# Two layer borders of a four-layer convolution kernel: the last image's stores, its norm, and the pools' waits

## Chip, cores and metric

The kernel runs on one core of a Trainium2 chip, as one launch. The metric is device time in microseconds (us) of one execution; lower is better. Before the change, three runs gave 5763.12, 5770.26 and 5770.41 us, median 5770.26.

TensorE is called PE below (its weight loads PEld), VectorE DVE, ScalarE ACT, GpSimd POOL; SP is the engine whose queue issues nearly all of this kernel's transfers (DMAs).

## The reference

Four layers run one after the other on x of shape 32 x 96 x 56 x 56 (images, channels, rows, columns), in float32. Each takes the group norm of x (32 groups of 3 channels, over the 3 channels and all pixels of one image), applies a block, and adds the result to x:

```python
def _gn(v, G=32, eps=1e-5):
    ...
    m = jnp.mean(g, axis=(2, 3, 4), keepdims=True)
    s = jnp.var(g, axis=(2, 3, 4), keepdims=True)
    return ((g - m) / jnp.sqrt(s + eps)).reshape(v.shape)
...
x = x + _L0_conv_ref(_gn(x), ...)   # 1x1 to 576 channels, SiLU, 3x3 depthwise, SiLU, squeeze-excite, 1x1 to 96, + identity
x = x + _L1_conv_ref(_gn(x), ...)   # 5x5 depthwise plus three Haar wavelet levels, each with 5x5 depthwise, and inverse
x = x + _L2_conv_ref(_gn(x), ...)   # 4-bit quantized: 1x1 to 576, 3x3 depthwise, 1x1 to 96
x = x + _L3_conv_ref(_gn(x), ...)   # 9x9 depthwise with diffusion kernels
```

## The kernel before, in words

**Two kinds of layer.** Layers 0 and 2 go image by image: an image is a tile of 96 channels (partitions) by 3136 pixels, two images stand side by side in a pair tile `xt` of 25 KB a partition. Layers 1 and 3 go channel by channel: a channel's tile `X` holds all 32 images, with 112 partitions for row and phase in each of two halves and 16 more for the rows beside them (`load_halves`, L657). Depthwise filters become products with banded matrices: `raw` is read from memory and put in order by ACT copies into `T` (L666, L694). So at the two borders 0 to 1 and 2 to 3 the data change from images to channels through memory (`y0`, `y2`), in six arrays of 16 channels each (GR = 16). No channel can be read before the last image of its group of 16 is stored; and the factors of the group norm (a row of 32 scales, 32 offsets and a bias for each channel) need the statistics of all 32 images.

**The end of layers 0 and 2.** `store_images` (L159) stores two images at once, one DMA for each group of 16 channels. The last image is stored by tiles: four tiles of 14 rows, six groups, 24 DMAs of 49 KB (`store_tile`, L152), issued by `add` (L495, L1171) when a tile's residual is added. A row piece of one image is 14 floats, 56 B. Then `store_norm` (L95) makes the factors for all 32 images: statistics of the last image (layer 0: ACT sums with an accumulator, L309, and L508 to L524; layer 2: `bn_stats` on DVE, L87), group means by a product with `S.grp` on PE (L106), variances by a second (L111), a power on POOL (L113), and the row is stored in memory by SP (L119).

**The beginning of layers 1 and 3.** `layer1` (L710) loads constants, lets POOL clear its T3, T2 and c2 tiles (L749), and runs over 48 pairs of channels; iteration i loads pair i + 3 (`load`, L752: X, the norm row `nr` broadcast to all partitions, raw, raw2 and T3), prepares pair i + 2 (`normal`, `matrices1`, `matrices2`, `high`, `low`), takes pair i + 1 through the small wavelet levels (`lowest1`, `lowest2`, `level3`, `level2`), and finishes pair i (`level1`, L835: two coarse and three fine matmuls into one PSUM tile for each half, then DVE adds and SP stores to `y1`). `layer3` (L1247) does the same with single channels, loading four ahead (AHEAD), preparing two ahead, and filtering the current one with three matmuls a half (`filtered`, L1280).

**What sets the order.** In layers 0 and 2 the order of PE, DVE and ACT work is written out by hand (L62, L68: a letter for each step, `-` and `+` for an image earlier or later), while SP's and POOL's order is chosen by the compiler's scheduler. In the loops of layers 1 and 3 SP's order is that of the program too (`MANUAL_SP`). Every engine works through its queue in order, so a waiting instruction holds all that stands behind it.

**Memory.** Each layer takes its tiles from pools that are opened when it begins and closed when it ends, so a later layer's pools lie where those of an earlier one lay. Before the change, the first use of the new pool's space waits for the whole of what was there. In layer 0 the pair of images 30 and 31 lies in `pairs[1]` (L546); layer 2 begins its own pairs in `Layer2` (L890), which also prepares its weights while layer 1 runs (`behind`, L1348).

## Time and profile before

| what | value |
|---|---|
| median of the runs | 5770.26 us (5763.12 to 5770.41) |
| the profiled execution | 5772.8 us, of which the profile's span is 5771.0 us |
| busy in the span: PE, DVE, ACT, POOL | 5488.4, 4689.3, 4184.5, 239.8 us |
| mean granted PE clock | 0.982 of full speed |
| HBM read and written | 284.44 and 214.08 MB |
| chain of work that ended last, by engine | PE 82%, DMA 5%, ACT 4%, issue 3%, DVE 3%, SP 1%, POOL 1% |

The page cuts the span into 40 slices of 144 us; a digit is the busy share in tenths:

```profile
PE   5999999999999999995999999999999999997999
...
PEclk9999999999999999997999999899999999998999
DMA  3122333332222233216566666579688696845888
GB/s 99 17 56 59 63 57 59 57 58 56 42 54 54 58 59 58 47 20 66 142 148 148 148 148 113 21 53 50 42 52 46 51 54 42 53 28 35 241 254 245
```

From left to right: the start, layer 0 to slice 19, layer 1 to slice 25, layer 2 to slice 37, layer 3 to the end. PEclk is the clock that was granted to PE. The DMA row is the mean busy share of the 16 DMA engines. Rows of other views give a start, a length and what ran; a bracket at the end gives the idle time ahead of the instruction and what ended it. SPq rows are SP's queue: the length is the time that issuing took, not the transfer's.

### The profile page before, as it was taken

What the parts mean: (1) busy time and instruction counts of PE and PEld (TensorE: products, weight loads), DVE (VectorE), ACT (ScalarE), POOL (GpSimd) and SP (SyncE); (2) the same over time, 40 slices, a digit from 0 to 9 for tenths busy, and PEclk for the clock granted to TensorE, in tenths of its full rate; (3) what the DMA queues carried; (4) which work ended last, traced back from release to release, by engine and by line L of the source; (5) the groups of instructions that cost most, each with busy time, mean ns of one, the idle gap of its engine ahead of it and who ended that gap; (6) DMA issues with size and microseconds to landing.
All of it is one profiled execution on the core that took longest, in us unless ns stands there. A gap on an engine that the chain in (4) does not pass through costs nothing.

```text
span 5771.0 us, 137224 instructions
## 1 busy us (share of the span) xinstructions
PE 5488.4 (95%) x59688; PEld 3064.9 (53%) x59688; DVE 4689.3 (81%) x5388; ACT 4184.5 (73%) x6036; POOL 239.8 (4%) x156
## 2 busy tenths in 40 slices
PE   5999999999999999995999999999999999997999
PEld 2333333333333333332566665777788778775444
DVE  6999999999999999994776665777777777774777
ACT  5888888888888888874565554777777777774555
POOL 5000000000000000000000000000000000000000
PEclk9999999999999999997999999899999999998999
DMA  3122333332222233216566666579688696845888
GB/s 99 17 56 59 63 57 59 57 58 56 42 54 54 58 59 58 47 20 66 142 148 148 148 148 113 21 53 50 42 52 46 51 54 42 53 28 35 241 254 245
DMA packets 1306412, 454.32 MB, mean 79 GB/s; under 512 B 1123841, under 2 KB 1301753, under 8 KB 1303889
## 3 DMA queue, kind: packets, MB, share of 16 engines
q1 hardware_dynamic: 1305809, 445.54, 50.9%
q8 instruction: 468, 7.67, 0.6%
q14 instruction: 135, 1.11, 0.1%
HBM read 284.44 MB, written 214.08 MB: 86 GB/s over the span
## 4 chain that ended last, share of the span: by engine, by line
PE 82%; DMA 5%; ACT 4%; issue 3%; DVE 3%; SPq 1%; POOL 1%; POOLq 0%; ACTq 0%; DVEq 0%
PE psd L432 17%; PE psd L1131 12%; PE psj L483 11%; PE ps L365 7%; PE pc L842 7%; PE ps L1112 6%; PE pse L388 6%; PE pc L1285 4%; PE psj L1168 3%; PE pc L826 2%; ACT hi L1084 2%; PE pa L800 2%; DMA xt<-y 1%; PE pc L816 1%; DMA X<-y 1%
## 5 line engine op out<-in xcount | busy, mean ns | idle before, releaser
L406 DVE SCALAR_TENSOR_TENSOR h<-hpad,l_wdw,h 128x3136 f32<-128x3136 f32 x512 | 1782.3, 3481 | 9.1
L432 PE MATMUL psd<-plane,filt 128*32 128x392 f32 (+5 forms) x16384 | 1082.9, 485 | 0.0
L1131 PE MATMUL psd<-apad,diag 64*64 64x392 bf16 x20736 | 913.2, 329 | 68.3 <-issue 64.6
L1131 PEld LDWEIGHTS <-diag 64*64 64x64 bf16 x20736 | 686.4, 106 | 291.1 <-issue 114.7
L432 PEld LDWEIGHTS psd<-plane,filt 128*32 128x32 f32 (+1 forms) x16384 | 389.9, 108 | 674.4 <-issue 621.5
L672 ACT COPY T<-raw 32x112 f32<-32x112 f32 (+2 forms) x1440 | 463.0, 385 | 270.6 <-DMA raw<-tdiff 217.1
L1102 ACT ACTIVATE u<-ps,o,s 128x784 int16<-128x784 f32 x576 | 538.1, 1002 | 165.7 <-PE ps L1112 146.8
L1102 ACT ACTIVATE a<-psd,o,s 128x784 int16<-128x784 f32 x448 | 423.9, 998 | 273.7 <-PE psd L1131 273.7
L365 PE MATMUL ps<-xn,l_wboth 96*128 96x392 f32 (+1 forms) x1536 | 465.0, 505 | 23.9 <-ACT xn L347 23.0
L406 DVE SCALAR_TENSOR_TENSOR hc<-hhalf,l_wdw,hc 128x1568 f32<-128x1568 f32 x256 | 473.7, 1851 | 16.1 <-ACT hc L399 9.5
L1112 PE MATMUL ps<-hi,l_w1q 96*128 96x392 f32 x1280 | 467.3, 365 | 9.2 <-ACT hi L1084 9.2
L1285 PE MATMUL pc<-x,T 128*112 128x416 f32 (+1 forms) x1152 | 416.0, 524 | 41.9 <-DMA raw<-tdiff 40.0
L842 PE MATMUL pc<-x,T 128*112 128x416 f32 (+1 forms) x1152 | 445.4, 523 | 0.0
L1112 PE MATMUL ps<-lo,l_w1q 96*128 96x392 f32 x1280 | 442.7, 346 | 0.0
L388 PE MATMUL pse<-xn,l_wboth 96*32 96x392 f32 x4096 | 392.0, 501 | 3.6 <-ACT hab L409 3.6
L365 PEld LDWEIGHTS ps<-xn,l_wboth 96*128 96x128 f32 (+1 forms) x1536 | 219.0, 172 | 248.6 <-issue 59.8
L1285 PEld LDWEIGHTS pc<-x,T 128*112 128x112 f32 x1152 | 204.3, 178 | 253.0 <-issue 229.8
L409 ACT ACTIVATE hab<-psd,o,s 128x784 f32<-128x784 f32 x256 | 283.8, 1113 | 57.8 <-PE psd L432 54.8
L375 ACT ACTIVATE hpad<-ps,o,s 128x784 f32<-128x784 f32 x256 | 278.6, 1104 | 48.9 <-PE ps L365 47.5
L483 PE MATMUL psj<-h,wg 128*32 128x392 f32 x3072 | 307.1, 514 | 1.3 <-DVE wg L472 1.3
L483 PE MATMUL psj<-hab,wg 128*32 128x392 f32 x3072 | 304.1, 509 | 0.0
L392 ACT ACTIVATE plane<-pse,o,s 128x784 f32<-128x784 f32 x256 | 256.0, 1000 | 25.4 <-PE pse L388 20.4
(234 smaller groups left out, 7618.9 us busy)
## 6 DMA issues: line engine op xcount, KB each, us to landing
X<-y SPq DMA_DIRECT2D x192, 392.0 KB
y<-xt SPq DMA_DIRECT2D x180, 392.0 KB
xt<-in_x_dram SPq DMA_DIRECT2D x16, 2352.0 KB
y<-y SPq DMA_DIRECT2D x96, 392.0 KB
xt<-y SPq DMA_DIRECT2D x96, 392.0 KB
out_dram<-y SPq DMA_DIRECT2D x96, 392.0 KB
twav<-zwav SPq DMA_DIRECT2D x768, 36.8 KB
raw<-twav SPq DMA_DIRECT2D x96, 168.0 KB
```

What stands on the lines that cost most here:

```text
L365: nc.tensor.matmul(ps[p, j, :NT], wexp[:, k * 128 : k * 128 + 128][:, m], im["xn"][:, j, rows, :].rearrange("c h w -> c (h w)"), start=Tru ...
L388: nc.tensor.matmul(ps[f * GC : (f + 1) * GC, half, :NT].rearrange("p (r w) -> p r w", w=W2), wexp[:, c : c + GC], im["xn"][:, f % 2, r0 : ...
L406: nc.vector.scalar_tensor_tensor(h2, taken(im, k, t), wdw[:, k, t : t + 1], h2, ALU.mult, ALU.add)
L409: nc.scalar.activation(view, ps, AF.Silu, bias=bi[1][:, c : c + 1], scale=sc[1][:, c : c + 1], accum_out=accum)
L432: nc.tensor.matmul(ps[at * GC : (at + 1) * GC, r, :NT].rearrange("p (r w) -> p r w", w=W2)[:, r0 - half * n : r1 - half * n, q0:q1], filt[ ...
L483: nc.tensor.matmul(ps[s * GC : (s + 1) * GC, t, :NT].rearrange("c (m r q) -> c r q m", m=2, q=W4), wg[p, k, c * GC : (c + 1) * GC], phases ...
L672: nc.scalar.copy(to.rearrange("x t (p s) -> x t p s", p=NPH), v[:, k])
L842: nc.tensor.matmul(ps[:PH, to], st["T"][j][:, h, k, :], st["x"][:, j, h, of], start=False, stop=(n == NK - 1))
L1102: nc.scalar.activation(out, ps, AF.Identity, bias=o[:, c : c + 1], scale=s[:, c : c + 1])
L1112: nc.tensor.matmul(ps[:, j, :NT], w1[:, k * 128 : k * 128 + 128], im[part][:, r0 : r0 + RT, :].rearrange("c h w -> c (h w)"), start=(part ...
L1131: nc.tensor.matmul(ps[q, j, :NT].rearrange("p (r w) -> p r w", w=W), diag[p, k, t, :], v, start=(t == 0), stop=(t == 8))
L1285: nc.tensor.matmul(ps[:, :, to], st["T"][:, h, k, :], st["x"][:, h, :, of], start=(n == 0), stop=(n == NK - 1))
```

## The change

It does five things, at both borders where not said otherwise.

- **Stores.** Of the last image's 24 store DMAs, those of channel group 0 are issued first (in layer 0 two of them, in layer 2 three, by `add`; the rest of group 0 ahead of the next layer's first X). All others are kept in a list (`LastStores`) in the order of the groups, and `left.issue(n)` takes n of them from it between the next layer's loads: 2 and then 3 in each `load` of layer 1; 1 and then 2 behind each channel's loads, from channel 2 on, in layer 3.
- **Norm.** `store_norm` becomes a class `Norm`: the factors of images 0 to 30 (EARLY) are made while the last image is still worked on, those of image 31 (LATE) at the end. In layer 0 the last image's statistics are taken by `bn_stats` on DVE, tile by tile, in place of the ACT sums; in layer 2 they are taken tile by tile too. The row is stored by `made.store` within the next layer's loads.
- **Pair 0 of layer 1.** Its matrices are loaded before its images. A new `begin` prepares it in one piece and lets PE make its fine matmuls at once; its `level1` then adds only the coarse ones. Iteration -2 does nothing beside it. The constants are loaded inside the loop's hand-set order. In layer 3 the matrices of channels 0 and 1 are loaded first.
- **Memory.** The pair tile with the last image and the norm row stay in a pool of their own (`kept`) through layers 1 and 2, where they serve as layer 2's first pair and its norm row. The three sets of T3, T2 and c2 are placed in reverse.
- **Waits.** The pools of layers 1, 2 and 3 are opened with `reuse_waits="tile"`: a tile of a new pool waits for the tiles that lay where it lies, not for the whole pool.

The diff, cut to its core (left out: signatures, the other pools' same argument, the unpacking of names):

```diff
+def tile_stats(nc, st, x, i):
+
+    for j in (2 * i, 2 * i + 1):
+        nc.vector.bn_stats(st[:, j, :], x[:, j * RT * NPH : (j + 1) * RT * NPH, :])
+
+
+EARLY, LATE = slice(0, B - 1), slice(B - 1, B)
+
+
+class Norm:
+
+
+    def __init__(self, nc, S, room, row, mv, bias):
+        self.nc, self.S, self.mv, self.bias = nc, S, mv, bias
+        self.d, self.dv, self.ve = (room[:C, i * B : (i + 1) * B] for i in range(3))
+        self.row = row[:C]
+
+    def slices(self, at):
+        return [t[:, at] for t in (self.d, self.dv, self.ve, self.row[:, :B])]
+
+    def means(self, at):
+        self.nc.vector.tensor_copy(self.slices(at)[2], self.mv[:, at, 0])
+
+    def centred(self, at, ps):
+
+        nc = self.nc
+        d, dv, ve, _ = self.slices(at)
+        ps = ps[:C, 0, : d.shape[-1]]
+        nc.tensor.matmul(ps, self.S.grp, ve, start=True, stop=True)
+        nc.vector.tensor_tensor(d, ve, ps, ALU.subtract)
+        nc.vector.tensor_tensor(dv, d, d, ALU.mult)
+        nc.vector.tensor_tensor(dv, dv, self.mv[:, at, 1], ALU.add)
+        nc.vector.tensor_tensor(d, ve, d, ALU.subtract)
+
+    def deviations(self, at, ps):
+
+        nc = self.nc
+        _, dv, ve, rstd = self.slices(at)
+        ps = ps[:C, 1, : ve.shape[-1]]
+        nc.tensor.matmul(ps, self.S.grp, dv, start=True, stop=True)
+        nc.vector.tensor_scalar(ve, ps, EPS_GN, None, ALU.add)
+        nc.gpsimd.tensor_tensor(rstd, ve, self.S.mhalf[:C, : ve.shape[-1]], ALU.pow)
+
+    def begin(self):
+        if self.bias is None:
+            self.nc.vector.memset(self.row[:, 2 * B :], 0.0)
+        else:
+            self.nc.vector.tensor_copy(self.row[:, 2 * B :], self.bias)
+        self.means(EARLY)
+
+    def last(self, ps):
+        self.means(LATE)
+        self.centred(LATE, ps)
+        self.deviations(LATE, ps)
+        self.nc.vector.scalar_tensor_tensor(self.row[:, B : 2 * B], self.d, -1.0, self.row[:, :B], ALU.mult, ALU.mult)
+
+    def store(self, dram):
+        self.nc.sync.dma_start(dram, self.row)
...
+def store_tile(nc, y, xt, i, g):
 
     rows = slice(i * 2 * RT * NPH, (i + 1) * 2 * RT * NPH)
-    for to, of in groups(im["xt"][:, rows], y, lambda y: y[:, rows, im["b"], :], store=True):
+    for to, of in groups(xt[:, rows], y, lambda y: y[:, rows, B - 1, :], store=True, of=[g]):
         nc.sync.dma_start(to, of)
+
+
+class LastStores:
+
+
+    def __init__(self, nc, y, xt, first):
+        self.left = [(lambda i=i, g=g: store_tile(nc, y, xt, i, g)) for g in range(C // GR)
+                     for i in range(NP) if g or i in first]
+
+    def issue(self, n):
+        for store in self.left[:n]:
+            store()
+        del self.left[:n]
...
         im["wg"] = wg
+        if im["b"] == B - 1:
+            norm.begin()
         nc.vector.tensor_tensor(im["wg"], wproj, im["gate"].unsqueeze(2).to_broadcast([128, ND, C]),
                                 ALU.mult)
+        if im["b"] == B - 1:
+            norm.centred(EARLY, pn)
...
+        if (im["b"], i) == (B - 1, 0):
+            norm.deviations(EARLY, pn)
...
-                        store_tile(nc, y0, im, 2 * t + a)
+                        tile_stats(nc, stats, im["xt"], 2 * t + a)
+                        if a == 0:
+                            store_tile(nc, y0, im["xt"], 2 * t, 0)
 
...
     def store(im):
+        if im["b"] == B - 1:
+            nc.vector.bn_aggr(mv_all[:, B - 1, :], stats.rearrange("c a b -> c (a b)"))
+            norm.last(pn)
+            return
...
-    cp = ctx.enter_context(tc.tile_pool(name="l1c", bufs=1))
+    cp = ctx.enter_context(tc.tile_pool(name="l1c", bufs=1, reuse_waits="tile"))
...
+    sets = [None] * NF
+    for i in reversed(range(NF)):
+        sets[i] = {
+            name: cp.tile(shape, dtype, tag=f"{name}{i}", name=f"{name}{i}") for name, shape, dtype in (
+                ("T3", [2 * HH, 2, HH * KW], F32), ("T2", [PH, 2, NK, 128], F32), ("c2", [128, 2, 2, N2, B], F32R))}
+    for d in sets:
+        for t in d.values():
+            nc.gpsimd.memset(t.bitcast(F32) if t.dtype == F32R else t, 0.0)
...
+        if i == 0:
+            for c in range(2):
+                matrices(c)
+            left.issue(2)
+            made.store(norm)
+            for part in (images, factors):
+                for c in range(2):
+                    part(c)
+            return st
+        for c in (2 * i, 2 * i + 1):
+            images(c)
+            factors(c)
+            matrices(c)
+        left.issue(3)
...
+    def fine(st, j, h, first):
+        ps = st["pf"][j, h]
+        for n, (k, to, of) in enumerate(shifts(W4, NK)):
+            nc.tensor.matmul(ps[:PH, to], st["T"][j][:, h, k, :], st["x"][:, j, h, of],
+                             start=first and n == 0, stop=not first and n == NK - 1)
+
+    def coarse(st, j, h, first):
+        ps, rows = st["pf"][j, h], slice(128 if first else PH)
+        for n in range(2):
+            nc.tensor.matmul(ps[rows, n::2, :], up1[:, h, n, rows], st["c2"][:, j, h],
+                             start=first and n == 0, stop=not first and n == 1)
...
+        if st["i"]:
+            st["pf"][j, h] = pfine.tile([128, W4, B], F32, tag="f", name="pc1")
+            coarse(st, j, h, True)
+            fine(st, j, h, False)
+        else:
+            coarse(st, j, h, False)
...
+    def begin(st):
+        for j in range(2):
+            matrices1(st, j)
+        for j in range(2):
+            matrices2(st, j)
+        for j in range(2):
+            for h in range(2):
+                normal(st, j, h)
+                st["pf"][j, h] = pfine.tile([128, W4, B], F32, tag="f", name="pc1")
+                fine(st, j, h, True)
+            high(st, j)
+        for j in range(2):
+            low(st, j)
...
+        low1 = rounded("low1", [128, 2, 2, 128])
+        up1 = rounded("up1", [128, 2, 2, 128])
+        low2 = constant("low2", [PH, 2, 2 * HH])
+        up2 = constant("up2", [2 * HH, 2, 128])
         for i in range(-3, PAIRS):
             nxt, far = i + 1, i + 2
             if i + 3 < PAIRS:
                 sts[i + 3] = load(i + 3)
+            if far == 0:
+                begin(sts[0])
+                continue
...
+        self.pairs = [kept, cp.tile([128, H * NPH, 2, W4], F32, tag="xt1", name="xt1")]
...
+        if (im["b"], h) == (B - 1, 0) and k in (2, 4):
+            (norm.centred if k == 2 else norm.deviations)(EARLY, bank(name="pr"))
...
-            store_tile(nc, y2, im, i)
+            if i < NP - 1:
+                store_tile(nc, y2, im["xt"], i, 0)
+            tile_stats(nc, parts, im["xt"], i)
 
     def store(im):
         b = im["b"]
+        if b == B - 1:
+            nc.vector.bn_aggr(mv_all[:, B - 1, :], parts.rearrange("c a b -> c (a b)"))
+            norm.last(bank(name="pl"))
+            return
...
+        if b == B - 2:
+            norm.begin()
...
-        for c in range(AHEAD):
-            load(c)
-            load_norms(c)
+        for c in range(2):
+            matrices(c)
+        left.issue(1)
+        images(0)
+        made.store(norm)
+        images(1)
+        load_norms(0)
+        for c in range(2, AHEAD):
+            images(c)
+            matrices(c)
+            left.issue(2)
         for c in range(-2, C):
             if 0 <= c < C - AHEAD:
                 load_norms(c + AHEAD)
-                load(c + AHEAD)
+                images(c + AHEAD)
+                matrices(c + AHEAD)
+                left.issue(2)
...
+        def keep():
+            pool = ctx.enter_context(tc.tile_pool(name="kept", bufs=1, side="right"))
+            row = pool.tile([128, 2 * B + 1], F32, tag="row", name="row")
+            return pool.tile([128, H * NPH, 2, W4], F32, tag="kept", name="kept"), row
```

## The prediction, written before the changed kernel was run

> **What bounds the kernel now.** I read the page first: TensorE (PE) is busy 5488 of 5771.0 us, and most slices of the PE row are full; the dips stand at the start, near slice 19 and near slice 37, which are the two borders that the change touches. So the question is only how long PE stands still there. The profiled execution took 5772.8 us (span 5771.0, 1.8 us around it), 2.5 us above the median 5770.26; my savings are differences, so I subtract them from the median.
>
> Next the chain of work that ended last, around the border of layers 0 and 1 (start, length, what; us):
>
> ```profile
> 2639.55 21.34 PE psj L483 x230
> ...
> 2685.72 2.46 SPq L156
> ...
> 2688.28 6.51 DMA norm<-hc
> ...
> 2697.02 3.12 DMA nr<-norm
> ...
> 2700.26 0.93 DVE x L775
> ...
> 2710.57 3.00 PE pa L800 x7
> ...
> 2729.70 2.98 PE pa L800 x7
> ...
> 2750.13 1.73 PE pa L800 x7
> ...
> 2768.16 1.71 PE pa L800 x7
> ```
>
> Projection ends at 2660.9. Then SP issues stores until 2688.2, writes the norm row, and only at 2700.26 can VectorE (DVE) normalise channel 0. The last four lines are the same step (lowest band) of pairs 0 to 3: intervals 19.1, 20.4, and then 18.03, the steady PE-bound period. Layers 2 and 3, SP's rows of the timeline:
>
> ```profile
> 5299.47 33.27 SPq L156 DMA_DIRECT2D y<-xt  x21
> 5332.84 0.92 SPq L119 DMA_DIRECT2D norm<-room  x1
> 5339.32 0.31 SPq L660 DMA_DIRECT2D X<-y  x1
> ...
> 5342.50 0.42 SPq L1264 DMA_DIRECT2D nr<-norm  x1
> ```
>
> and GpSimd's (POOL) and DVE's rows there:
>
> ```profile
> 5308.46 5.44 POOL L113 TENSOR_TENSOR room<-room,mhalf 96x32 f32<-96x32 f32 x1 [106.24 <-DVE room L112]
> ...
> 5313.93 0.19 DVE L114 SCALAR_TENSOR_TENSOR room<-room 96x32 f32<-96x32 f32 x1 [5.55 <-POOL room L113]
> 5346.67 0.62 DVE L1277 TENSOR_TENSOR x<-X,nr 128x448 f32<-128x448 f32 x1 [32.55 <-DMA nr<-norm]
> ```
>
> The row is ready at 5314.1 but its store starts at 5332.84, behind the 24 tile stores: making the norm earlier is worth nothing here unless the stores move too. The stages (us; PE, PEld, DVE, ACT, POOL busy; clock, DMA share, GB/s) say what layer 3 can bear:
>
> ```profile
> 5336.00:5338.00 2.00, 0.00 (x0) 0.00 (x0) 0.00 (x0) 0.00 (x0) 0.00 (x0) 0.50 0.02 2
> 5338.00:5340.00 2.00, 0.00 (x0) 0.00 (x0) 0.00 (x0) 0.00 (x0) 0.00 (x0) 0.50 0.00 0
> ...
> 5400.00:5500.00 100.00, 100.00 (x281) 49.46 (x280) 78.98 (x136) 53.70 (x157) 0.00 (x0) 1.00 0.86 250
> ```
>
> The last store's data stop by 5336.4 and X may start at 5339.3: a receipt of some 2.8 us. Steady layer 3 is PE-bound (12 matmul records a channel, 281 in 100 us: 4.27 us a channel) with DMA at 0.86.
>
> **Layers 0 to 1, step by step.**
> (a) *Norm of 31 images ahead.* Two copies run on DVE while it waits for the sigmoid (0.3 us gap before the gate product), the first group matmul beside that product. The second stands between projections 0 and 1: like the row at L111, 0.5 us on PE's path. The 31-column power (5.4 us on POOL) ends by 2654, hidden behind projections 1 and 2.
> (b) *Statistics by tile.* The ACT sums (16 instructions) go; DVE gets 8 bn_stats (0.48 us, from the row at L91: 3.83 for 8) and one aggregate (0.37). Half lie under projection 2. Adds end near 2663.5; then 4 x 0.48 + 0.37 = 2.3, then the one-column norm: copy to second matmul's reader 2.3 (L105 to L112, 5306.08 to 5308.38), power of one column 0.55 with handovers (L1062), the row 0.2: 3.1. Row ready at 2669, before 2677.4.
> (c) *Stores.* 22 of 24 move into layer 1: 2 before X, 3 in each of seven loads. Ahead of them on SP now stand 4 constants and 10 matrix loads, 14 x 0.43 = 6 us, from about 2659 (two tile stores remain behind add 1): to 2665. Two stores to 2668, their receipt (2.8) to 2671; the row's store goes out at 2669 and is behind the same wait. X(0), X(1): 3.4 us, to 2674.4; the norm has landed, two row reads; the first took 3.1 us to land: DVE starts at 2678. Before 2700.3: 22 us earlier.
> (d) *Pair 0 begun apart.* ACT's matrix copies are done by then. DVE needs 1.55 us (0.92 + 0.63) per normal, PE 3 matmuls for each: 2.15 us at full clock, 4.3 at half. Here a rule is weighed. Layer 3's opening starts at half clock at 5348.2 and shows 1.00 from 5353; the Trainium skill, "TensorE: Matmul & The Clock Gate", Part 1, puts release after a window of some 3.4 us of sustained work. But the chain's stretch 2717 to 2727.6 (small matmuls of 56 and 112 rows, gaps under 1 us) stayed at 0.50 for ten us. By the page pair 0's small levels after the begin run at full clock (about 3 us less); by that row at half. I let the begin's full-array matmuls warm PE after 4.4 us (fine matmuls 2679.6 to 2691) and take 2 us of the 3. Lowest band of pair 0: 2691 (19.8 earlier); of pair 1: 2708, ACT-bound (17 us instead of 19.1). Iteration 0 then has only the coarse matmuls, 9.4 us of PE; ACT (12.3 us of rows a pair) with its handovers makes it 15.5 instead of 20.4. Saved: 21.7 + 4.9 = 27 us.
> (e) *The seven loads with 3 stores.* SP issues about 10 us per pair now, +4.2 is 14 of 18; DMA 0.65 + 4.2/18 stays below 0.9. Covered; nothing queued behind is needed within that iteration.
>
> If POOL runs the memsets of T3 behind the last power, SP stands at the T3 load until 2668.6 and with it the second channel's loads, stores and X: 5.5 us lost. If they sit earlier (set 0 lies where h2 and filters ended early), nothing. I take nothing.
>
> **Layers 2 to 3.**
> (f) Adds and statistics alternate: 1.08 + 0.98 us a tile against PE's 1.66, from 5295.8: end 5304, aggregate 5304.4, one-column norm 3.1, and 1 us for two extra banks that PE must await between depthwise blocks (not shown before; between 0 and 2): row at 5308.5. SP: three stores have gone out by 5302, six matrix loads 2.6 us, the fourth store, receipt: X(0) at 5309.3; row store, X(1); the row read waits for the norm's landing, until 5314.3, and lands after 4.1 us (5342.50 to 5346.6): PE at 5320 instead of 5348.2, 28 us earlier.
> (g) *20 stores then stand among layer 3's loads*, two behind each of channels 2 to 11, and everything behind them on SP (the next X, matrices, the output) waits. Price: a store took 1.38 us in the 24 (33.2 / 24), its DMA share 0.68, so between 0.94 (DMA work only, if its gaps can be filled) and 1.4; in layer 2, four times as large ones beside loads had median 6.36, 1.6 a piece. The skill speaks otherwise by bytes: "DMA: Bandwidth & Descriptors", Anatomy of one DMA, gives about 2 us fixed, which overlaps, plus bytes over 436 GB/s (a fit for another issue path): 49 KB would move in 0.11 us and 20 stores in 2. Its Specifications do say that runs under 512 B miss line rate; these are 56 B. I take the row: 1.4. SP: X, halos and matrices 3.5, output 0.4, stores 2.8: 6.7 us a channel instead of 3.9. X(2) at 5315, X(12) at about 5381; its matrices land, are copied (2.4) and PE has channel 12 at about 5389 (9.5 us after X, as channel 1 of before: 5342.96 to 5352.5, less 1.5 as there is no cold queue). Before: 5348.2 + 12 x 4.27 + 3 cold = 5402.4. So of 28 us about 13 remain; with DMA as the limit (2.35 loads, 1.4 output, 2.8 stores, 6.55 a channel) 17. I take 15: the difference moved from idle PE to PE waiting for X. After channel 11 SP needs 3.9 of 4.27, so no more is lost, and none regained.
>
> **Edits at nothing:** both3, the kept pair, pairs' loads of layer 2 (first needed 300 us after the last store). Tile waits in layers 1 to 3: they free the early matrix loads (counted above); at layers 1 to 2 the first image waits for the last y1 store (2.9 us) and its own load (9.2), true dependences. But SP could now put third-pair loads (6.5 us each, L1016) ahead of that load: 0 to 10 lost. I take 0.
>
> Sum: 27 + 15 = 42 of 5770.3: **5728 us**.
>
> **The rivals.**
> 1. *The stores are nearly free among large loads* (0.9 us or less). For: DMA share 0.68 while they ran alone. Against: 1.6 in layer 2. Layer 3 keeps 25 to 28: 5716. Chance 0.18.
> 2. *SP is held*: memsets behind the power (5.5), tile waits that don't free the matrix loads (8 + 6), or third-pair loads ahead at layers 1 to 2 (up to 10). The changed waits then don't do what they say. 5742. Chance 0.2.
> 3. *Nothing measurable*: the idle time comes back whole in both openings: 5765. Chance 0.03.
> 4. *Slower*: the small stores among loads cost far more than alone, in layer 3's first twelve channels. Each us above 1.4 costs 20 us; the 42 are gone at 1.4 + 42/20 = 3.5 us a store. At 4.0, 5780. Against: the longest single one was 3.1 and the median beside loads 1.6. Chance 0.03.
> Likeliest 0.56.
>
> **How the numbers follow.** The likeliest case spans 5718 to 5738 (layer 3 between 7 and 21, layer 1 between 24 and 30). The range 5708 to 5748 takes in cases 1 and 2. About 0.2% (11 us) is what a measurement tells from no change: faster 0.94, same 0.03, slower 0.03.
>
> **What would show it.** Row ready 8 us (layer 0) and 5.5 us (layer 2) earlier; DVE's first normal of layer 1 near 2678; first pc of layer 3 near 5320 and then PE idle some 13 us in its first 55 us, waiting for X or matrices, with two stores per channel on SP at 1.4 each; no PE idle of that kind in pairs 1 to 7. Wrong if SP's stores there take 0.4 (rival 1), if X(0) waits for matrix loads (2), or if layer 2's first image is later after the last y1 store.

## The result and the profile after

| | before | after |
|---|---|---|
| median of the runs, us | 5770.26 (5763.12 to 5776.03, 5 runs) | 5745.4 (5743.2 to 5755.46, 5 runs) |
| ratio, 95% interval | | 0.9962 (0.9947 to 0.9976) |
| span of the profiled execution, us | 5771.0 | 5744.5 |
| PE busy, us | 5488 | 5496 |

Faster by 22 us (14 to 31), where 42 was forecast. A later set of runs gave 0.9953 (0.9938 to 0.9967), so 22 to 27 us it is. The two profiled executions differ by 26.5 us. PE does the same work; it stands still for less time. I go through the stages in the order of the prediction.

**Layers 0 to 1.** The chain of work that ended last, around this border (start, length, what):

```profile
2679.11 5.02 DMA nr<-norm
...
2684.25 0.93 DVE x L855
...
2685.97 11.26 PE pc L918 x24
2697.23 1.68 PE pa L880 x8
...
2713.02 2.99 PE pa L880 x7
...
2730.57 2.98 PE pa L880 x7
...
2750.76 1.73 PE pa L880 x7
```

The first normal (L855) stands at 2684.25, 16.0 us earlier than 2700.26, not 22. The last four lines are the lowest band of pairs 0 to 3. The third (2730.57) is 19.6 us earlier than its partner 2750.13, but the fourth 17.4 (2768.16 less 2750.76): the interval from pair 2 to pair 3 is now 20.2 us and no longer 18.03. Of "27" 17.4 are there, and layer 1 ends 17.1 earlier (3575.7, before 3592.8). Why the normal is late shows in SP's rows of the timeline and POOL's:

```profile
2661.20 0.42 SPq L827 DMA_DIRECT2D raw<-twav  x1
2668.30 0.31 SPq L829 DMA_DIRECT2D T<-twav  x1
...
2670.97 0.90 SPq L189 DMA_DIRECT2D y<-kept  x2
2671.97 0.81 SPq L152 DMA_DIRECT2D norm<-row  x1
2675.54 0.30 SPq L727 DMA_DIRECT2D X<-y  x1
```

```profile
2667.46 0.54 POOL L136 TENSOR_TENSOR row<-xt,mhalf 96x1 f32<-96x1 f32 x1 [14.16 <-DVE xt L135]
2667.95 1.00 POOL L810 MEMSET T<- 56x280 f32 x2
```

```profile
2668.03 0.19 DVE L149 SCALAR_TENSOR_TENSOR row<-xt,row 96x32 f32<-96x32 f32 x1 [0.66 <-POOL row L136]
```

SP stands 6.7 us at its first load into T3 (L829), until POOL has cleared that tile; POOL clears it only after the last power, though it stood idle for the 14.16 us ahead of that power. The row itself was ready at 2668.2 (forecast 2669), but its store is issued at 2671.97, behind that load.

**Layer 2's end and the border to layer 3.** SP's and DVE's rows there:

```profile
5292.18 0.32 SPq L727 DMA_DIRECT2D X<-y  x1
...
5294.02 0.38 SPq L152 DMA_DIRECT2D norm<-row  x1
...
5296.85 0.34 SPq L1393 DMA_DIRECT2D nr<-norm  x1
```

```profile
5291.77 0.19 DVE L149 SCALAR_TENSOR_TENSOR row<-room,row 96x32 f32<-96x32 f32 x1 [0.66 <-POOL row L136]
5300.93 0.63 DVE L1408 TENSOR_TENSOR x<-X,nr 128x448 f32<-128x448 f32 x1 [8.98 <-DMA X<-y]
```

Of the 25 us from the row (before 5313.93) to X (5339.32) nothing is left: X goes out 0.4 us behind the row. (The bracket at L1408 names X, which had gone out 8.7 us before; the read of the row, nr, went out 4.1 us before.) From layer 2's last `add` (start 5287.1; before 5301.3) to layer 3's first matmul it is 15.3 us where it was 46.9.

**Layer 3's opening** in stretches (us, busy PE, PEld, DVE, ACT, POOL; clock, DMA share, GB/s), the fourth line for comparison with the one shown of before:

```profile
5330.00:5340.00 10.00, 8.76 (x24) 3.81 (x22) 4.20 (x8) 2.65 (x8) 0.00 (x0) 1.00 0.72 187
5340.00:5350.00 10.00, 5.64 (x8) 2.59 (x9) 4.47 (x8) 2.85 (x9) 0.00 (x0) 0.66 0.72 158
5350.00:5360.00 10.00, 8.94 (x26) 4.22 (x25) 5.95 (x11) 4.31 (x13) 0.00 (x0) 1.00 0.73 193
...
5400.00:5500.00 100.00, 99.71 (x279) 49.08 (x278) 79.79 (x139) 55.28 (x161) 0.00 (x0) 1.00 0.88 257
```

PE waits again in the second of these stretches, among the late stores. Outputs 0 to 10 leave SP 6.02 us apart (before 4.35); the lead over the kernel before is 41.8 us at output 0 and 24.9 at output 8. From the first matmul to the last output sum layer 3 takes 437.6 us (before 417.9).

### The profile page after: what moved, and what is told of

The parts are those of the page before. It is cut to its first block, busy times and chain, and to the rows that moved or that the text cites. A ratio compares the mean times of both kernels' runs of the same rounds, so it can differ in the third digit from the quotient of the medians.

```text
span 5744.5 us, 137240 instructions
## 1 busy us (share of the span) xinstructions
PE 5495.9 (96%) x59696; PEld 3060.6 (53%) x59696; DVE 4696.0 (82%) x5406; ACT 4173.3 (73%) x6020; POOL 239.8 (4%) x158
## 4 chain that ended last, share of the span: by engine, by line
PE 81%; DMA 6%; ACT 5%; DVE 3%; issue 2%; SPq 1%; POOL 1%; ACTq 0%; DVEq 0%; POOLq 0%
PE psd L482 17%; PE psd L1250 13%; PE psj L537 10%; PE ps L415 7%; PE ps L1231 7%; PE pc L918 7%; PE pse L438 6%; PE psj L1289 4%; DMA X<-y 3%; DMA raw<-tdiff 2%; ACT hi L1203 2%; PE pc L906 2%; PE pa L880 2%; PE pc L896 1%; ACT u L1221 1%
## 5 line engine op out<-in xcount | busy, mean ns | idle before, releaser
L918 PE MATMUL pc<-x,T 128*112 128x416 f32 (+1 forms) x1152 | 447.9, 525 | 18.8 <-DVE x L856 18.8
L1416 PEld LDWEIGHTS pc<-x,T 128*112 128x112 f32 x1152 | 204.7, 179 | 243.8 <-issue 200.5
L918 PEld LDWEIGHTS pc<-x,T 128*112 128x112 f32 x1152 | 192.0, 179 | 165.5 <-issue 165.5
```

Of the source, the lines that this page charges most:

```text
L918: nc.tensor.matmul(ps[:PH, to], st["T"][j][:, h, k, :], st["x"][:, j, h, of], start=first and n == 0, stop=not first and n == NK - 1)
L1416: nc.tensor.matmul(ps[:, :, to], st["T"][:, h, k, :], st["x"][:, h, :, of], start=(n == 0), stop=(n == NK - 1))
```

## The experiments

Every ratio is to the kernel before, on the same chip. Each diff shows only the core of its edit, and comments in it are notes for the reader. One execution's layer 2 varies by some 30 us between profiles (1570 to 1600 from its first projection to its last expansion, in 20 profiles of kernels that do the same there), more than most of these edits are worth; so I read each from its own stage.

**e1 and e2: stores ahead, and the same number of small ones.** My theory after the trace was that the number of DMAs is what hurts. The program's list of SP's instructions (names shortened) shows what each waits for: eight semaphores in turn, so that no DMA is issued before the one eight places ahead of it has landed. The traces agree: in layer 3 of all 20 profiles each DMA of SP waits for the semaphore that the one eight places before it set:

```
L727 DMACopy X<-y2 112x2x448 [waits DMAHW3,PE]
L730 DMACopy X<-y2 16x1x448 [waits DMAHW4]
L730 DMACopy X<-y2 16x1x448 [waits DMAHW5]
L755 DMACopy raw<-tdiff 128x336 [waits DMAHW6]
L756 DMACopy raw<-tdiff 16x336 [waits DMAHW7]
L757 DMACopy raw<-tdiff 16x336 [waits DMAHW0]
L189 DMACopy y2<-kept 16x56x14 [waits DMAHW1]
L189 DMACopy y2<-kept 16x56x14 [waits DMAHW2]
L1447 DMACopy out<-y 112x2x448 [waits DMAHW3,DVE]
```

With nine DMAs a channel the output waits for the X issued at the head of the same iteration.

```diff
-        left.issue(1)
+        left.issue(21)
         images(0)
```

> Control for the next run: the 20 late tile stores of layer 3 stand ahead of its first load again, the rest is as in the changed kernel. Both theories of the loss in layer 3 say the same: the first matmul some 27 us later than the changed kernel's 5302.4 (20 stores at 1.38), so near 5330, which is 18 us before 5348.2 of the kernel before; then outputs 4.3 us apart at once, the lead over the kernel before stays within 3 us from the first output to the last. Time about 5753.

Measured 0.9984 (0.9975 to 0.9992): first matmul 40.9 us behind layer 2's last add (after: 15.3), so the 20 stores cost 25.6 us there, 1.28 each; outputs 4.35 apart at once, layer 3 415.7 us. The control stands.

```diff
+            for store in left.again[:2]:    # the same stores, 2 rows of 56
+                store()
```

> The control plus 20 repeats behind the loads of channels 2 to 11, two each as in the changed kernel, but of 2 rows of a tile instead of 56: a 28th of the data, the same number of DMAs. Theory of the eight: SP may not issue a DMA before the one eight places earlier has landed, and with nine DMAs a channel the output waits for the X issued in the same iteration; then outputs of channels 0 to 8 are about 6 us apart and 12 to 18 us of the lead are lost, nearly as in the changed kernel. Theory of the prediction (each store costs 1.4 us of DMA work): the data are gone, so no more than 2 us are lost against the control.

Measured 0.9997 (0.9989 to 1.0006): outputs 0 to 10 are 5.09 apart, layer 3 420.6. Outputs are 0.74 us further apart and layer 3 loses 5 us, a quarter of the 20; neither theory had that figure. The matmul records (twelve a channel) show where the 5 us go. In the first twelve channels PE does not wait at all (54.0 us, e1 54.5). What goes is SP's lead: at channel 12 X goes out 6.9 us ahead of PE's start on it, in e1 14.6. From there to the end PE takes 366.5 us, in e1 361.1.

**e3 and e4: the same bytes in fewer DMAs.**

```diff
-                left.issue(2)
+                left.issue(1)      # each store now holds two tiles
```

> The changed kernel with the 20 late stores of layer 3 as 10, each of two neighbouring tiles, one per channel: the same bytes in the same runs of 56 B over the same ten channels, eight DMAs a channel instead of nine. Theory of the eight: the output no longer waits for the X of its own iteration, but X still for the X before it, so outputs are about 5.2 us apart; layer 3 loses some 8 to 11 us of the lead of 46 instead of 19; time about 5735. Theory of DMA work: nothing changes, loss 19, time 5745.

Measured 0.9974 (0.9963 to 0.9986), outputs 0 to 10 6.22 apart, layer 3 432.5.

```diff
-    nc.sync.dma_start(raw[LOW:PH, 1], t[c, LOW:PH])
-    nc.sync.dma_start(raw[PH:, 1], t[c, 128:])
+    nc.sync.dma_start(raw[LOW:, 1], t[c, LOW:].rearrange("(a x) k -> a x k", x=PH - LOW)[::2])
```

> As the run before, and the two small loads of a channel's matrices as one DMA (in layers 1 and 3), so seven DMAs a channel in layer 3's opening, as many as the kernel before has there without any store. Theory of the eight: outputs about 4.5 us apart from the start, layer 3 loses at most 5 us of the lead; time about 5729. Theory of DMA work: loss still near 19, time 5743 to 5745.

Measured 0.9953 (0.994 to 0.9965), but outputs 0 to 10 are still 5.86 apart. With nine, eight and seven DMAs a channel the opening has nearly one pace, so there the theory of the eight falls. The pace agrees with the prediction's (6.55 to 6.7 us a channel forecast, 5.9 to 6.4 measured), but that the bytes at the DMA engines set it is not shown: their share is 0.72 to 0.77 in these openings. What SP's row of e4 shows is that issuing itself takes longer behind such a store:

```profile
5324.33 0.41 SPq L189 DMA_DIRECT2D y<-kept  x1
5324.85 2.49 SPq L1446 DMA_DIRECT2D out_dram<-y  x1
```

The output behind a two-tile store takes SP 2.6 us in the mean of eight (2.3 in e3, 0.4 in e1), and in one case (5331.63 to 5334.77) nothing that it could have waited for ended meanwhile. In e4 issuing fills 5.9 of 6.3 us a channel, in the changed kernel 5.2 of 6.5, in e1 3.4 of 4.4. Why issuing slows behind these stores stays open.

As a whole e4's layer 3 takes 424.2 us, 8 less than e3's: 62.7 against 66.1 to channel 12, and 361.4 against 366.3 from there. So the merging paid mainly after the stores, and the time is the one that the theory of the eight had forecast, by another way.

**e5 and e13: the stores spread over layer 3.**

```diff
-                left.issue(2)
+                if c % 4 == 3:
+                    left.issue(1)
```

> The changed kernel with the 20 late stores of layer 3 one behind every fourth channel (3, 7, ... 79) instead of two behind each of channels 2 to 11. Theory of DMA work: a store costs about 1 us of the queue beyond what is free, but steady layer 3 leaves some 0.13 of 4.3 us a channel free, 2.2 us in four channels, more than one store's 1.0 to 1.4; so outputs are 4.4 us apart from the start and layer 3 takes some 418 us from its first matmul to its last instead of 437; time about 5727 (19 less than the changed kernel). Rival, that a store costs a fixed stall wherever it stands (20 at about 1 us): layer 3 takes 435, time as the changed kernel.

Measured 0.9978 (0.9969 to 0.9987): layer 3 446.5, worse than the changed kernel's 437.6. The stretch, and the waits of SP in it (total, times, longest):

```profile
5400.00:5500.00 100.00, 90.86 (x241) 43.07 (x240) 69.06 (x121) 47.83 (x141) 0.00 (x0) 0.97 0.79 228
```

```profile
SPq L730 <- DMA X<-y: 6.4, 10, 1.0
...
SPq L727 <- DMA y<-kept: 2.9, 1, 2.9
```

The DMA engines are less busy than before (0.79) and PE waits 9% of the time: free share on the DMA engines is not free room for a store. One wait is of my making: the next group's X stood directly behind its last store.

```diff
-                if c % 4 == 3:
+                if (c + AHEAD) % 16 in (2, 5, 8, 11):
```

> As e5_spread, but each group's four stores stand behind its channels 2, 5, 8 and 11 of 16, so that the last has landed long before the next group's first X, which in e5 stood behind it. If that wait is what e5 paid, the spacing of outputs in channels 10 to 80 falls from 4.82 to 4.5 or less and first to last matmul of layer 3 from 446 to 425 or less. If a store costs its 1.2 us or more wherever it stands in SP's row, the spacing is still 4.65 or more and layer 3 takes 436 to 442.

Measured 0.9958 (0.9943 to 0.9973), outputs 10 to 80 4.70 apart, layer 3 440.5. Without the group wait layer 3 is 6 us shorter; the rest stays, more than 1 us a store.

**e9 and e14: the stores on POOL's queue.**

```diff
+            with tc.issue_after(made.power.ins):
+                left.issue(2)       # by nc.gpsimd.dma_start
```

> The changed kernel with the 20 late stores of layer 3 issued by POOL, which has nothing else to do there, behind the last power; the same bytes in the same runs of 56 B, but nothing of them in SP's row, which has seven DMAs a channel again. Theory of the queue: a store is dear because SP stands behind it (its issue, and then the DMA eight places on, which waits for its landing), so layer 3 from first to last matmul takes 412 to 420 us (before 411.6, changed kernel 437.1), time about 5725. Theory of DMA work: the stores crowd the loads on the DMA engines from whichever queue, so layer 3 still takes 432 or more, time about 5742; between the two, the part that falls is the queue's.

Measured 0.9965 (0.9952 to 0.9978). POOL issued them all at the border:

```profile
5288.36 6.85 POOL L189 DMA_DIRECT2D y<-kept  x9
5295.88 0.73 POOL L189 DMA_DIRECT2D y<-kept  x1 [0.66 <-DMA y<-kept]
```

Layer 3 takes 420.4, but begins 27.9 us behind layer 2's last add instead of 15.3: the price is paid at the border.

```diff
+            if cur and c % 3 == 0 and left.left:
+                turn = nc.gpsimd.tensor_copy(pace, cur["y"][:1, 1, 0, :1])
+                with tc.issue_after(turn.ins):
+                    left.issue(1)
```

> The changed kernel with the 20 late stores on POOL's queue, one behind every third channel from 0 to 57 (POOL copies one element of that channel's output first, so that it waits for it). Theory that SP stands behind a store's landing: nothing of it is left, layer 3 takes 412 to 420 us, and its first matmul is 17 us after layer 2's last as in the changed kernel; last projection to last matmul of layer 3 near 433 instead of 449 to 455. Theory of data on the DMA engines: as dear as e5 or e13, layer 3 takes 430 or more.

Measured 0.9922 (0.9905 to 0.994); layer 3 430.8, outputs 10 to 80 4.60 apart. Cheaper than in SP's row (440.5), but not free: 15 us above e1, with nothing of the stores in SP's row. SP standing behind a landing is not the whole cause.

**e17: spread in SP's row, with one DMA less a channel.** e13 with the merging of e4.

> e13 (one store behind channels 2, 5, 8, 11 of each 16, in SP's row) and the two small matrix loads of a channel as one DMA (layers 1 and 3). If the number of DMAs a channel in a row that may have only eight open is what leaves no room, six and a quarter leave it: outputs 4.4 us or less apart in channels 10 to 80, layer 3 from first to last matmul 414 to 422 us. If it was the store's place in SP's row that e15 took away, layer 3 stays at 430 or more.

Measured 0.9927 (0.9902 to 0.9952): layer 3 418.9, first matmul to last output sum, against 440.5 without the merging and 415.7 with no store in it at all (e1):

```profile
5400.00:5500.00 100.00, 100.00 (x281) 49.49 (x280) 79.00 (x137) 54.70 (x160) 0.00 (x0) 1.00 0.85 253
```

PE is full, and the same 20 stores cost 3 us where they had cost 25 (outputs are 4.44 apart, 4.4 or less was expected). So a row of seven DMAs a channel has no slack at 4.3 us. Even with no store in it, in e1, SP waits there at the first halo load, which stands eight places behind the X of the channel before:

```profile
SPq L730 <- DMA X<-y: 8.7, 14, 1.1
```

What gave the slack is not settled. Merging takes away three things at once: one of the eight open places, some 0.3 us of SP's issuing a channel (3.4 us in e1, 3.1 in e12), and one small load at the DMA engines. Only the first was in the theory, and no run separates them.

Layer 3 of these runs side by side (spacing of outputs 0 to 10 and 10 to 80; how far X goes out ahead of PE's first matmul on its channel, at channels 12 and 80; first matmul to last output sum):

| late stores in layer 3 | DMAs a channel on SP | 0 to 10 | 10 to 80 | X ahead at 12, 80 | us |
|---|---|---|---|---|---|
| none (before; e1) | 7 | 4.35; 4.35 | 4.43; 4.37 | 14.1, 7.7; 14.6, 10.3 | 417.9; 415.7 |
| two a channel (after; again) | 9 | 6.02; 6.38 | 4.40; 4.42 | 7.0, 7.7; 7.1, 7.6 | 437.6; 441.3 |
| the same, 2 rows each (e2) | 9 | 5.09 | 4.36 | 6.9, 7.5 | 420.6 |
| one of two tiles (e3; merged, e4) | 8; 7 | 6.22; 5.86 | 4.36; 4.26 | 7.0, 7.3; 6.7, 10.1 | 432.5; 424.2 |
| spread (e5; e13) | 7.25 | 4.63; 4.65 | 4.82; 4.70 | 12.4, 6.2; 12.9, 7.7 | 446.5; 440.5 |
| spread, merged (e17) | 6.25 | 4.43 | 4.44 | 13.7, 7.8 | 418.9 |
| POOL, spread (e14; merged, e15) | 7; 6 | 4.52; 4.36 | 4.60; 4.34 | 13.4, 8.3; 15.4, 11.5 | 430.8; 415.4 |

About 7 us (6.2 once, in e5) is the least lead in all of them; at that, PE waits for X and goes at SP's pace. With seven DMAs a channel and no store SP is a little slower than PE (e1: X 4.36 us apart, PE 4.30 a channel, channels 12 to 80), so its lead shrinks from 14.6 to 10.3 without PE noticing. With six it grows (e4 after its stores) or shrinks more slowly (e12, from 11.9 to 10.4).

**e6: T3's loads behind the row reads.**

```diff
-            for part in (images, factors):
+            for part in (images, factors, blocks3):
```

> The changed kernel with pair 0's two loads of T3 moved on SP from among its matrices to behind its row reads. Theory: SP stood at the first of them from 2661.6 to 2668.3 for POOL's memset, which POOL ran only behind the last power; without that the row is stored at about 2668.5 instead of 2672.0, X goes out before 2672, the row read at about 2672.7, and the first normal stands near 2677.5 instead of 2684.2; the gain passes on to pair 3 (lowest band near 2744 instead of 2750.8); time about 6 us less. Rival, that the row's landing and X are what hold it and SP's stand is covered: first normal at 2682 or later, less than 2 us gained.

Measured 0.9949 (0.9931 to 0.9967). SP's rows:

```profile
2664.07 0.96 SPq L189 DMA_DIRECT2D y<-kept  x2
2668.38 0.32 SPq L152 DMA_DIRECT2D norm<-row  x1
2668.80 0.37 SPq L727 DMA_DIRECT2D X<-y  x1
...
2672.43 0.92 SPq L772 DMA_DIRECT2D nr<-norm  x2
```

First normal 2676.4, 7.8 earlier; pair 3 at 2744.1, 6.7 earlier. The row's store now waits for the row alone. T3's loads thus cost 7.8 us at the first normal, where the prediction had priced them at 5.5.

**e10: pair 0 without its own beginning.**

```diff
-            if far == 0:
-                begin(sts[0])
-                continue
```

> The changed kernel without the separate beginning of pair 0 in layer 1 (pair 0 goes through the loop's order, as before the change). The prediction put the beginning at some 5 us (iteration 0 at 15.5 instead of 20.4) and more with a warm clock: then pair 3's lowest band stands 5 us later than in the changed kernel, near 2756. Theory after the result: the fine matmuls taken ahead delay the lowest band of pair 0 by about as much as they spare later, so pair 3 is at 2751 to 2753.5 (up to 2.5 us later).

Measured 0.9953 (0.994 to 0.9966): first normal 2684.0, pair 3's lowest band 2751.5. The beginning is worth about 1 us.

**e8: PE kept busy in layer 1's opening.** It adds matmuls whose result is overwritten at once (the like stands ahead of level 3 of pairs 0 and 1, not shown).

```diff
+        if st["i"] in (1, 2):
+            for _ in range(5):
+                nc.tensor.matmul(ps, low1[:, 0, 0, :], st["xh"][:, :, 0, 0::2, :], start=True, stop=True)
```

> The changed kernel with matmuls whose result is overwritten at once: 5 ahead of the lowest band of pairs 1 and 2, 7 ahead of level 3 of pairs 0 and 1, sized to fill the gaps of 1.8 to 2.1 us in which PE waits there. Theory that the gaps drop PE's clock: it stays at 1.00 from 2696 to 2735, level 2 and the lowest bands take half, and pair 3's lowest band comes 5 to 8 us earlier (2743 to 2746 instead of 2750.8). Rival, that small matmuls (56 and 112 rows) hold the clock down whatever stands between them: still 0.5 to 0.7 there, pair 3 at 2750 to 2752.

Measured 0.995 (0.9933 to 0.9967), of which nothing is in layer 1: pair 3 at 2750.7. Stretches of the changed kernel and of e8:

```profile
2714.00:2720.00 6.00, 5.13 (x18) 3.46 (x17) 2.64 (x4) 3.87 (x10) 0.00 (x0) 0.65 0.39 76
2720.00:2726.00 6.00, 6.00 (x23) 4.72 (x22) 5.22 (x7) 4.76 (x14) 0.00 (x0) 0.63 0.51 140
```

```profile
2714.00:2720.00 6.00, 4.91 (x25) 3.78 (x25) 3.10 (x5) 3.81 (x10) 0.00 (x0) 0.88 0.37 82
2720.00:2726.00 6.00, 5.42 (x29) 4.04 (x27) 5.21 (x7) 4.77 (x14) 0.00 (x0) 1.00 0.57 148
```

In these 12 us the clock rose to 0.88 and 1.00 and level 2 took 3 us less, but pair 3 did not move. Ahead of pair 2's lowest band PE then waited longer for DVE, whose subtraction makes xl, and began it at 2729.93, only 0.6 us earlier:

```profile
2729.93 0.74 PE L883 MATMUL pa<-xl,low1r 128*128 128x448 f32 x1 [2.36 <-DVE xl L867]
```

From 2726 to 2738 the clock was 0.75 and 0.68, near the changed kernel's 0.50 and 0.73, and the matmuls of the lowest bands still took 0.57 us. The expected 1.00 from 2696 to 2735 was not reached, so what a full clock at the lowest bands is worth was not tested. Both theories bet on the clock, and neither asked whether DVE ends the wait.

**e7: layer 2's early norm in unused columns.**

```diff
-            (norm.centred if k == 2 else norm.deviations)(EARLY, bank(name="pr"))
+            (norm.centred if k == 2 else norm.deviations)(EARLY, parts[-1][1][:, :, NT:])
```

> The changed kernel with the two early norm matmuls of layer 2 written into the unused columns of the depthwise tile just filled (392 to 511) instead of taking a bank each from the ring of four. Theory: the two extra banks cost PE some 6 us of the last image (36 us from the last expansion to the first projection instead of 30) because the next depthwise pair must take a bank that is still being evicted; so the stretch is 30 to 31 us, time about 5 us less. Rival, that DVE's and POOL's norm work beside the depthwise evictions is what slows it: stretch stays at 35 to 36.

Measured 0.9958 (0.9943 to 0.9972). From the last expansion to the last add it takes 41.8 us; the changed kernel's first profile has 45.9, but in thirteen other profiles of the same layer 2 it is 39.6 to 41.8. The 45.9 belonged to that one execution, and this theory to a single profile. The edit gains nothing.

**e11, e12, e15: edits together.** All have e6's and e7's edits and the merged matrix loads; e11 has two-tile stores in SP's row, e12 e9's stores, e15 e14's.

> Three edits together on the changed kernel: T3 loads behind the row reads, layer 2's early norm in the depthwise tile's unused columns, and layer 3 with stores of two tiles and the small matrix loads as one DMA. If they add up: first normal of layer 1 near 2677, 4 us in layer 2's tail, 13 us in layer 3; about 24 us below the changed kernel, ratio to the kernel before near 0.992. If what is won early is lost in layer 3 (a border that waits for something else): ratio 0.995.

Measured 0.9949 (0.9937 to 0.9961): layer 1 as e6 (first normal 2677.0), but layer 3 430.5 where e4 had 424.2. A miss.

> As the run before, but layer 3's 20 late stores single and on POOL's queue. Theory of the queue: layer 3 at 405 to 412 us from first to last matmul, some 10 us better than the run before, ratio near 0.990. Theory of DMA work: no better than the run before or worse, ratio 0.992 to 0.994.

Measured 0.9942 (0.993 to 0.9955): layer 3 415.5, begun 28.6 us behind layer 2, as in e9. The ratio is that of the theory of DMA work, the length of layer 3 neither's (405 to 412 was the queue's).

> e14 with the three other edits: T3 loads behind the row reads, layer 2's norm in the depthwise tile, the small matrix loads as one DMA. If e14 holds: 7 (layer 1) + 4 (layer 2) + 18 to 22 (layer 3) below the changed kernel, ratio to the kernel before near 0.990. If the stores' data count: ratio 0.994.

Measured 0.9894 (0.9879 to 0.9909), median 5717.4, layer 3 415.4 us, begun 17.0 behind layer 2's last add. It beats both kernels: by medians of the same chip the kernel before by 58 us and the changed one by 34:

> The changed kernel itself, for its time and its layer 3 on the same chip: ratio to the kernel before 0.995 to 0.9975, last projection of layer 2 to last matmul of layer 3 between 449 and 455 us.

Measured 0.9953 (0.9938 to 0.9967). From the last projection to the last matmul it takes 460.0 us, above the expected range. Counted, as in the rest of this text, from layer 2's last add to the last output sum, it is 458.4; the six profiles with this layer 3 have 447.9 to 458.4, mean 451.6.

> The kernel before, profiled a second time. If the late rise of PE's clock in layer 2's opening (0.50 for 22 us of back-to-back matmuls) belongs to that one execution, the stretch from layer 2's first matmul to its first projection is 50 to 55 us as in the changed kernels, not 57.2; if it is the kernel's own, 56 to 58. Layer 3 from first matmul to last output sum 415 to 420 us either way, pair 3's lowest band 67 to 69 us behind the first normal of layer 1.

Measured 5775.1, beside 5767.9 of the same kernel. First matmul of layer 2 to first projection 53.4 us, so the 57.2 was that execution's clock. Last add to last output sum 457.2 (464.8 in the first profile), mean 461.0.

## Why the prediction missed, by its steps

Its time was 5728, its range 5708 to 5748. The measured ratio makes 5748 of the median of before, the very edge: little more than half of the saving came.

- **(a), (b) right.** Row of layer 0 ready at 2668.2 (forecast 2669).
- **(c) the failed step.** "DVE starts at 2678 ... 22 us earlier": 16.0. The prediction saw the mechanism ("If POOL runs the memsets of T3 behind the last power, SP stands at the T3 load until 2668.6"), priced it at 5.5 us and took nothing for it; SP stood until 2668.30. Worth at the first normal: 7.8 us (e6). With the loads moved the normal is at 2676.4, 24 us earlier, so the rest of the step's sum holds. The rival "SP is held" had this part right.
- **(d) wrong in size.** "4.9" more by iteration 0, besides the warm clock: pair 3 has gained 17.4 us where the normal had gained 16.0. Iteration 0 did fall from 20.4 to 17.6 (forecast 15.5), but the fine matmuls taken ahead (11.26 us) let pair 0's lowest band gain only 13.3, and 2.2 us are lost again in the interval from pair 2 to pair 3, 20.2 us for 18.03. Without `begin` it is the same within 1 us (e10). Those 2.2 us are the low clock (0.50 in 2726 to 2732, 0.73 in 2732 to 2738, then 1.00): pair 2's lowest band and the six fine matmuls behind it take 6.18 us, pair 3's 4.02. In the kernel before, the clock reached 1.00 at about the same time, but one pair earlier in the order, so its interval ran at 1.00 throughout:

```profile
2733.75 3.07 PE L918 MATMUL pc<-x,T 128*112 128x448 f32 x6
...
2752.55 2.31 PE L918 MATMUL pc<-x,T 128*112 128x448 f32 x6
```

Of the two ways that the prediction weighed, the row of before was right: the clock was 0.5 to 0.7 between pairs 0 and 2 after the begin's full-array matmuls too, so the 2 us taken for a warm clock did not come.
- **(e) right.** Three stores take SP 2.0 us a load there; pairs from the fourth on keep 18.0 us.
- **(f) right.** "28 us": 31.6 from the last add in these two profiles; 25 to 32 with the repeats (before 46.9 and 41.7, after 15.3 and 17.1). The two banks, 1 us forecast: the tail is 39.6 to 41.8 us against 38.6 and 37.7, but without the banks (e7) it is 41.8, so what these 2 us are stays open.
- **(g) right up to channel 12, wrong behind it.** X(2) to X(12) took SP 65.8 us (forecast 66), PE had channel 12 7.0 us after X(12) (forecast 8), and from the first matmul to channel 12 it is 67.7 us, before 54.0: 13.7 lost, where "13" was forecast (in the six profiles with this layer 3 12.2 to 17.2). What failed is the last sentence, "After channel 11 SP needs 3.9 of 4.27, so no more is lost": 6.0 us more are lost from channel 12 to the end (369.9 us, before 363.9; the six profiles 364.4 to 370.0, mean 367.9; e18 361.5, e1 361.1). With its waits SP needs not 3.9 but 4.36 us a channel in e1, more than PE's 4.30; in the changed kernel, which comes out of the stores with X only 7.0 us ahead instead of 14.1, PE goes at SP's pace from there (4.42). So of 31.6 us at this border 11.9 remain (464.8 less 452.9), or 9.4 by the means 461.0 and 451.6; the forecast was 15. Against the control e1 the 20 stores cost 17 to 26 us in the six profiles, 0.8 to 1.3 each, so "nearly free" and "slower" fall with it.

Two readings in (g) are wrong. The row of 33.27 us holds 21 stores, not 24, so 1.58 us each; all 24 took 35.8 us, 1.49 each. And 5352.5 in the kernel before is the second half of channel 0; channel 1 begins at 5354.86, 11.9 us after its X. That the 8 us taken from it came near the measured 7.0 is luck.

Sum, measured in the two profiles: layer 1 17.1, layer 2's opening 4.9 (scatter of the clock, e18) and middle -0.5, its tail -7.3 (mostly scatter, e7), border and layer 3 11.9: 26.1 of the 26.5 seen. Against the forecast of 42 that is 10 us too few in layer 1 (6 in (c), 3.5 in (d)) and 3 to 6 in layer 3.

By the fit of the Trainium skill ("DMA: Bandwidth & Descriptors", Anatomy of one DMA) 20 such stores would move in some 2 us, an estimate by its figure; measured are about 20 us, so the row of 56 B runs was the right one to take. What remains open: what holds pairs 0 and 1 (DVE's subtraction ahead of the lowest band ended two of the waits, 2.1 and 1.7 us; taking it ahead was not tried), why SP issues more slowly behind these stores, and which of the three things that merging frees made room in e17; the number of semaphores itself could not be changed.

## What to carry to other kernels

When a change moves a wait, list every instruction that still stands ahead on the same queue, and price a hazard that you can name: this one was named, priced at 5.5 us and left out. Before putting transfers "into the gaps", see whether the queue that issues them is faster than the engine it feeds: here X's lead over PE shrank even without a store, and free share on the DMA engines was worth nothing until one small DMA a channel was merged away. A lead once lost does not come back on such a queue. And read an edit of a few us from its own stage in several profiles, never from one.

## What the runs showed of the hardware that I had not expected

- DVE's copy of 128 x 512 to the rounded format took 5.36 us in the changed kernel (2668.14 to 2673.50), while POOL's memsets ran (2667.95 to 2673.2); with no POOL work beside it, before, 0.43 us. The Trainium skill ("SBUF — State Buffer") describes the port pair of the two as a lock that blocks the loser. Here the copy lay across six memset groups in a row, in the changed kernel, e1 and e6 alike; that the lock is the cause is not shown, since no run moved the memsets away. The last memset, the two copies of the changed kernel, and the same copy before:

```profile
2672.38 0.84 POOL L810 MEMSET c<- 128x896 f32 x1
...
2668.14 5.36 DVE L799 CAST low1r<-low 128x512 fp32r<-128x512 f32 x1
2673.42 0.41 DVE L799 CAST up1r<-up 128x512 fp32r<-128x512 f32 x1
...
2695.10 0.43 DVE L732 CAST low1r<-low 128x512 fp32r<-128x512 f32 x1 [17.68 <-DMA low<-in_low_dram]
```

- PE's clock at layer 2's opening rose after about 24 us of back-to-back matmuls in the first profile of before, after about 10 in its second, and after 4 to 11 in the changed kernels: 5 us that no edit made.
- Twenty 49 KB stores in runs of 56 B, crowded into ten channels, cost layer 3 17 to 26 us (six profiles, 432.2 to 441.3, against e1's 415.7), and 17 as ten DMAs of two tiles (e3): 0.8 to 1.3 us a tile either way. Alone they took SP 1.28 (e1) to 1.49 us each (before).
